# Spreading scores through DRAM, row sums by a column of ones, and a re-laid instruction order in a four-layer graph network

## The chip, the cores and the metric

The kernel runs on one core of one Trainium2 chip. The metric is device time in microseconds (us), from the start of the program to its end. A core has engines that each run their own queue of instructions in order and meet through semaphores: TensorE (PE, matrix products into PSUM; PEld are its weight loads), VectorE (DVE), ScalarE (ACT), GpSimd (POOL) and SyncE (SP, which here issues every DMA).

## The reference, cut to what matters

There are 128 graphs of 64 nodes with 512 features, all in float32. Four layers follow each other; each normalizes x, applies a ReLU, runs a graph layer on the result h, and adds it to x.

```python
h = relu(layernorm(x));  x = x + hypergraph_conv_twice(h, adj)          # layer 0, W1 512->1024, W2 1024->512
h = relu(layernorm(x))                                                   # layer 1
s = (h @ w) @ a
A = s[..., :, None] + s[..., None, :]
A = tanh(A / 8) * 8;  A = where(A >= 0, A, 0.1 * A);  A = exp(A) * adj
A = A / A.sum(-1, keepdims=True) * adj.sum(-1, keepdims=True)
x = x + A @ h @ w
h = relu(layernorm(x))                                                   # layer 2
weight = adj * exp((h @ Wq.T + bq) @ (h @ Wk.T + bk).T)
x = x + weight / weight.sum(2, keepdims=True) @ (h @ Wv.T + bv)
h = relu(layernorm(x))                                                   # layer 3
e = leaky_relu(sj[:, None, :] + si[:, :, None] + ab, 0.2)                # sj, si: h times two vectors
t = normalize_rows(adj * exp(e))
x = x + relu(sum over k of (t^k h) @ Wk[k] + bk[k])                      # k = 0, 1, 2
```

## The kernel before

**Tiles and groups.** Two graphs of 64 nodes fill the 128 partitions, and four such tiles (T = 4) are one group; there are NG = 16 groups. Small matrices of a group (adjacency, attention weights) are held in packed form, 128 x 4 x 64, or spread into block-diagonal 128 x 128 tiles ("bd") that a product can use. Layers 0 and 1 run over all 16 groups first, x then goes to DRAM (tensors xm), and layers 2 and 3 run over the 16 groups with other weights in the same memory (wa_mem, wb_mem).

**The large products.** They use a seven-product scheme (functions `strassen` and `seven`, products at L570 and L779): DVE combines operands (L562), PE forms seven products, ACT and DVE collect them in tiles U (L538, L540, L542), and a function of the layer evicts each result (for instance `scaled`, L588 and L590, for z in layer 0). Layers 0, 2 and 3 also transpose activations by an ACT copy into 16-bit planes, a DMA transpose (L519), and an ACT copy back (L520).

**Normalization.** `pre_ln` takes statistics on DVE (L489 to L491), a power on POOL (L492), one more small DVE operation (L499) and an ACT instruction (L500) that makes h. In layers 1 and 3 the four tiles h of a group are made once, multiplied with a vector for the scores (function `dot`, L358), and held until the softmax is done, when they are used again.

**Scores.** `bcast_sum` needs, for every pair of nodes of a graph, a row value plus a column value. It multiplies the column of values with an identity (dg, L605), lets PE sum over partitions with a block matrix of ones (ones_bd, L607), and adds the column to the result (L612). Layer 1 then forms the transposed attention matrix, and gets its row sums and those of the adjacency by two more products with ones_bd (L719), a reciprocal over 256 values per partition (L722) and a multiplication (L723), before it fills the block-diagonal tile PT (L725). Layer 2 gets its row sums by four one-column products (`col_sums`, L628), takes the reciprocal (L831), multiplies PT with the 512-wide value tile (L834), and scales and adds into x (L835). Layer 3 fills a transition tile tr (L858), transposes it (L863), squares it (L869), applies both powers to h (L883) and multiplies with three stacked weights.

**What sets the order.** Nothing is in program order. Every operation is entered in a graph (class `Graph`) with an engine, an estimated cost, its buffers and a due time (`prio`, advanced by `step`). `run` is a list scheduler: it goes through estimated time, starts on each engine what can start first, and among several the one with the lowest due time. It also picks the buffer slots. The instructions are then emitted in the order found, so each engine's queue is fixed when the kernel is built. The parameters are a stretch factor for each layer, a period for each loop, and a lead for the loads:

```python
STRETCH, PERIOD1, PERIOD2, LEAD = (1.65, 1.86, 2.69, 2.67), 80.0, 75.8, 1.5
```

The setup of layers 2 and 3 (Wq times Wk, L453 and L458; score vectors, L358 and L437) is entered with group 2 of the first loop. The estimate of a DMA is its size at 190 KB per us of queue time, and 2.0 us of latency.

Of the kernel before, what the change touches and what calls it, by code (L numbers as in the profile page):

```python
# [14 lines left out]
P = 128  # L15
C = 64
# [23 lines left out]
class Graph:  # L40
# [6 lines left out]
    def __init__(self):  # L47
        self.ops = []
        self.last_write, self.reads = {}, {}
        self.prio = 0.0  # L50

    def op(self, eng, cost, fn, r=(), w=()):
        o = Op()
        o.eng, o.cost, o.fn, o.prio = eng, cost, fn, self.prio
# [27 lines left out]
    def run(self, slots, after):  # L82
# [22 lines left out]
        while left:  # L105
# [42 lines left out]
            for q in o.succ:  # L148
                q.npre -= 1
                q.ready = max(q.ready, end if q.eng != o.eng else t + o.cost)  # L150
                if not q.npre:
                    open_[q.eng].append(q)
# [9 lines left out]
def tile_adj_preln_d4(  # L162
# [19 lines left out]
        "bd": ([P, T, P], 4), "dg": ([P, T, C], 1), "ee": ([P, T, C], 2),  # L182
        "st": ([P, 2, 6], 6), "mv": ([P, 2], 10), "ve": ([P, 1], 10), "rs": ([P, 1], 10), "nm": ([P, 1], 10),
        "col": ([P, T], 24), "ss": ([P, T, 2], 2),
# [6 lines left out]
        ([("s2", [P, 3, 4, P], 1), ("s1", [P, 3, 2, P], 2)], [("vu", [P, 2, D], 2), ("tt", [P, T, 2, P], 1)]),  # L191
# [57 lines left out]
    def c_v(n, from_psum=False):  # L249
        return n / 960 + 0.155  # L250
# [13 lines left out]
    def dma(kb, fn, r, w):  # L264
        return G.op("SP", kb / 190.0, fn, r, w)
# [4 lines left out]

    ident = const.tile([P, P], F32, name="ident")
    make_identity(nc, ident)
    ident2 = const.tile([P, C], F32, name="ident2")
    nc.vector.tensor_add(ident2, ident[:, :C], ident[:, C:])
    ones = const.tile([P, P], F32, name="ones")
    nc.vector.memset(ones, 1.0)
    ones_bd = const.tile([P, P], F32, name="ones_bd")
    nc.vector.memset(ones_bd, 0.0)
    for s in HALVES:
        nc.vector.memset(ones_bd[s, s], 1.0)  # L280
# [34 lines left out]
    xt, adjs, xmid = {}, {}, {}  # L315

    def load_group(g, src):
        b = Buf("adj")
        dma(256, lambda: nc.sync.dma_start(b.t, adj[g]), [], [b])
        adjs[g] = b  # L320
        for t in range(T):
            xx = Buf("x")
            at, key = src(g, t)
            dma(256, lambda xx=xx, at=at: nc.sync.dma_start(xx.t, at), key, [xx])
            xt[g, t] = xx
# [7 lines left out]

    G.prio = -1000.0
    load_group(0, x_in)
    load_w("w1", w1_sb, W1T)
    b1_b = [load_row(b1[i * D:(i + 1) * D]) for i in range(2)]
    gb2 = const.tile([P, KH, 2], F32, name="gb2")
    dma(8, lambda: nc.sync.dma_start(gb2[:, :, 0], gamma), [], ["gb2g"])
    dma(8, lambda: nc.sync.dma_start(gb2[:, :, 1], beta), [], ["gb2b"])  # L340
    load_w("w2", w2_sb, W2T)
    b2_b = load_row(b2)
    G.prio = 10.0
    load_w("w", w_sb, w)
    bq_c = load_cols("bq_c", bq, KD)
# [15 lines left out]
    def combine(name, w_, x_, kc, n, eng):  # L361
# [8 lines left out]
        G.op(eng, cost, lambda: sub(x_[:, 1], blk(1, 1), blk(0, 1)), [*low, *high], [(name, "x1")])  # L370
        G.op(eng, cost, lambda: sub(blk(0, 1), blk(0, 1), blk(0, 0)), [*low, (name, "x1")], [T1])
# [36 lines left out]
    def setup_l0():  # L408
# [6 lines left out]
        dve(0.2, lambda: nc.vector.tensor_scalar(gsc[:, :, 0], gb2[:, :, 0], 1.0 / DH, None, op0=ALU.mult), ["gb2g"], ["gsc0"])  # L415
        dve(0.2, lambda: nc.vector.tensor_copy(gsc[:, :, 1], gb2[:, :, 1]), ["gb2b"], ["gsc1"])
# [10 lines left out]
        for c in range(KH):  # L427
            dve(0.75, lambda c=c: nc.vector.scalar_tensor_tensor(
                w2_sb[:, c, :], w2_sb[:, c, :], gb2[:, c, 0:1], pm.t, op0=ALU.mult, op1=ALU.subtract),
                [pm, "gb2g"], [("w2", c // 2)])  # L430
# [9 lines left out]
    def setup_l1():  # L440
        wa, a_b = Buf("col"), temp(a.partition_broadcast(P))
        for c in range(KD):
            dot(lambda c=c: w_sb[:, c, :], lambda: a_b.t, lambda c=c: wa.t[:, c:c + 1], [("w", c // 2), a_b], [(wa, c)])
        spread(lambda: wa.t, lambda: wa_b.t, [(wa, c) for c in range(KD)], wa_b)

    def setup_l2():
# [3 lines left out]
        for o in range(KD):  # L450
            q_, k_ = temp(Wq[o * P:(o + 1) * P, :]), temp(Wk[o * P:(o + 1) * P, :])
# [8 lines left out]
            pe(c_mm(1, KD), mg, [k_, "bq_c"], [pg])  # L460
        for c in range(KD):
# [5 lines left out]
    def setup_l3():  # L467
        kk = Buf("mv")
        bv_t = temp(bv3.partition_broadcast(P))
        ab_t = load_tmp("rs", 1, lambda t: t, ab.partition_broadcast(P))  # L470
        for s in range(2):
            av, cc = temp(aw[s * D:(s + 1) * D].partition_broadcast(P)), Buf("col")
            dot(lambda: bv_t.t, lambda av=av: av.t, lambda s=s: kk.t[:, s:s + 1], [bv_t, av], [(kk, s)])
            for c in range(KD):
                wv = temp(Wv3[c * P:(c + 1) * P, :])
                dot(lambda wv=wv: wv.t, lambda av=av: av.t, lambda c=c, cc=cc: cc.t[:, c:c + 1], [wv, av], [(cc, c)])
            spread(lambda cc=cc: cc.t, lambda s=s: c3_b[:, s, :], [(cc, c) for c in range(KD)], ("c3", s))
# [7 lines left out]
    def norm_stats(src, k, r):  # L485
# [6 lines left out]
        pool(0.57, lambda: nc.gpsimd.tensor_tensor(rs.t, ve.t, mhalf, ALU.pow), [ve], [rs])  # L492
        return mv, rs

    def pre_ln(g, t):

        xx, nm, h = xt[g, t], Buf("nm"), Buf("h")
        mv, rs = norm_stats(lambda i: xx.t, 1, [xx])
        dve(0.16, lambda: nc.vector.scalar_tensor_tensor(nm.t, mv.t[:, 0:1], -1.0, rs.t, op0=ALU.mult, op1=ALU.mult), [mv, rs], [nm])  # L499
# [14 lines left out]
    def transposed(src, ksrc, planes, back, kback, dst, kdst):  # L514
# [4 lines left out]
        dma(200, lambda: nc.sync.dma_start_transpose(u16(back()).rearrange("p (b r) -> p b r", r=P), u16(planes.t)), [planes], kback)  # L519
# [64 lines left out]
    def scaled(dst, wdst, scale, ks, add, ka, p, u, v, n):  # L584

        if u is not None:
            (U, i), j, add0 = u, v[1], add
            dve(c_v(n), lambda: nc.vector.scalar_tensor_tensor(U.t[:, j], U.t[:, i], scale(), add0(), op0=ALU.mult, op1=ALU.add), [u, *ks, *ka], [v])  # L588
# [12 lines left out]

    def bcast_sum(col, row, r, extra=None):

        dg, p, z = Buf("dg"), Buf("ps"), Buf("ee")
        dve(0.42, lambda: nc.vector.tensor_mul(dg.t, ident2[:, None, :].to_broadcast([P, T, C]),  # L605
                                               row()[:, :, None].to_broadcast([P, T, C])), r, [dg])
        pe(c_mm(256, 1), lambda: nc.tensor.matmul(p.t[:, :T * C], ones_bd, dg.t.rearrange("p t c -> p (t c)"), start=True, stop=True), [dg], [p])  # L607
        if extra is not None:
# [3 lines left out]
        dve(0.42, lambda: nc.vector.tensor_add(z.t, p.t[:, :T * C].rearrange("p (t c) -> p t c", t=T),  # L612
                                               col()[:, :, None].to_broadcast([P, T, C])), [p, *r], [z])
# [8 lines left out]
    def col_sums(bd, r):  # L622

        p = Buf("ps")

        def mm():
            for t in range(T):
                nc.tensor.matmul(p.t[:, t:t + 1], bd.t[:, t, :], ones[:, 0:1], start=True, stop=True)  # L628
        pe(c_mm(1, T), mm, r, [p])
        return p  # L630


    def layer0(g):
        ad = adjs[g]
        AT = lambda: ad.t[:, 1]

        HT, mB, be, rb, pm, M = Buf("bd"), Buf("mB"), Buf("col"), Buf("col"), Buf("ps"), Buf("bd")
        for s in HALVES:
            dve(0.5, lambda s=s: nc.vector.tensor_scalar(HT.t[s, :, s], AT()[s], 0.0, None, op0=ALU.not_equal), [ad], [(HT, s.start)])
        dve(0.42, lambda: nc.vector.tensor_scalar(mB.t[:, :, :C], AT(), 0.0, None, op0=ALU.not_equal), [ad], [mB])  # L640
# [4 lines left out]
        dve(0.16, lambda: nc.vector.tensor_copy(mB.t[:, :, C:], AT()[:, :, 0:1]), [ad], [mB])  # L645
# [15 lines left out]
        for t0 in (0, 2):  # L661
            mh, zs, ys, rTs = [], [], [], []
            for t in (t0, t0 + 1):
                xx = xt[g, t]
                h = pre_ln(g, t)
                pool(1.3, lambda xx=xx, h=h: nc.gpsimd.tensor_add(xx.t, xx.t, h.t), [h, xx], [xx])  # L666
# [351 lines left out]
```

## Time and profile before

| | |
|---|---|
| time, median of 3 | 2472.81 us (2470.64 to 2474.09) |
| span of the profiled execution | 2471.6 us |
| mean granted TensorE clock | 0.992 |
| DMA moved | 163.39 MB, mean 66 GB/s |
| h made in all four layers (L500) | 256 instructions, 208.0 us busy on ACT |
| powers on POOL (L492) | 320 instructions, 202.2 us busy |

A group of instructions in the profile is a line of the kernel, an engine, an operation, what it writes and reads, its shape and count; then its busy time, the mean time of one, and after a second bar the idle time of the engine just before it, with what ended the idle time. A float32 matmul appears as two instructions. Matmuls overlap in the pipe, so the mean time of one is longer than what it adds to the span.

### The profile page before, as it was taken

How to read it: one execution, taken by the hardware profiler on the slowest of the kernel's cores; microseconds unless marked ns; L12 is line 12 of the kernel's file. 1: busy time of each engine (PE TensorE's matmuls, PEld its weight loads, DVE VectorE, ACT ScalarE, POOL GpSimd, SP SyncE). 2: the span in 40 equal slices, each digit the busy share in tenths (PEclk: the TensorE clock that was granted, in tenths of full speed). 3: DMA queues.
4: the chain of work that ended last, by engine and by line, in shares of the span. 5: the costliest groups of instructions: out<-in, count | busy, mean ns of one | idle time of the engine just before them, and what ended most of it. 6: DMA issues, size and time to landing. Idle time of an engine off the chain costs nothing.

```text
span 2471.6 us, 32994 instructions
## 1 busy us (share of the span) xinstructions
PE 2416.3 (98%) x12058; PEld 1878.4 (76%) x12058; DVE 1808.8 (73%) x4128; ACT 1176.1 (48%) x1626; POOL 723.9 (29%) x842
## 2 busy tenths in 40 slices
PE   8999999999999999999989999999999999999998
PEld 4566767776677776677777888888888888888886
DVE  8678888888888888888875566665566665566663
ACT  4355554655554555454633445343445343445321
POOL 3223344333444333444221212221212221212220
PEclk9989999999999999999999999999999999999998
DMA  5242222222222222222431233212223222222211
GB/s 187 68 103 52 60 59 66 73 56 49 63 64 61 73 56 52 60 69 56 120 111 46 58 69 69 69 43 61 55 69 73 61 48 60 56 69 67 58 22 34
DMA packets 323698, 163.39 MB, mean 66 GB/s; under 512 B 278096, under 2 KB 278096, under 8 KB 323536
## 3 DMA queue, kind: packets, MB, share of 16 engines
q1 hardware_dynamic: 323536, 161.28, 26.3%
q8 instruction: 95, 1.56, 0.3%
q14 instruction: 67, 0.55, 0.1%
HBM read 59.52 MB, written 34.60 MB: 38 GB/s over the span
## 4 chain that ended last, share of the span: by engine, by line
PE 86%; DVE 9%; ACT 2%; DMA 1%; issue 1%; POOL 0%; DVEq 0%; ACTq 0%; POOLq 0%
PE ps L570 56%; PE ps L779 15%; PE ps L509 3%; PE ps L883 2%; PE ps L834 2%; PE ps L697 2%; DVE s_s_vu_tt L562 2%; PE ps L804 2%; DVE rT_a L562 1%; DVE u L588 1%; PE ps L607 1%; DVE ee L722 1%; PE ps L869 1%; DVE z_hT L590 1%; ACT rT_a L520 1%
## 5 line engine op out<-in xcount | busy, mean ns | idle before, releaser
L570 PE MATMUL ps<-wb_mem,rT_a 128*128 128x256 f32 x2056 | 480.7, 382 | 8.1 <-ACT rT_a L520 4.5
L492 POOL TENSOR_TENSOR rs<-ve,mhalf 128x1 f32<-128x1 f32 x320 | 202.2, 634 | 919.9 <-DVE ve L491 841.3
L570 PEld LDWEIGHTS ps<-wb_mem,rT_a 128*128 128x128 f32 x2056 | 389.5, 191 | 80.6 <-issue 13.8
L500 ACT ACTIVATE h<-x,nm,rs 128x512 f32<-128x512 f32 x256 | 208.0, 815 | 319.0 <-DVE nm L499 309.0
L570 PE MATMUL ps<-wb_mem,s_s_vu_tt 128*128 128x256 f32 x1152 | 274.3, 381 | 1.2 <-DVE x L737 0.9
L570 PE MATMUL ps<-wb_mem,tmp_mB_s 128*128 128x256 f32 x1152 | 263.1, 380 | 0.0
L570 PEld LDWEIGHTS ps<-wb_mem,s_s_vu_tt 128*128 128x128 f32 x1152 | 219.0, 191 | 48.3 <-issue 14.4
L570 PE MATMUL ps<-wb_mem,mT_a 128*128 128x256 f32 x1016 | 246.8, 382 | 5.7 <-DVE y_qT L600 5.0
L570 PE MATMUL ps<-wa_mem,mT_a 128*128 128x512 f32 x512 | 244.5, 602 | 2.8 <-ACT mT_a L511 1.5
L570 PEld LDWEIGHTS ps<-wb_mem,tmp_mB_s 128*128 128x128 f32 x1152 | 217.8, 190 | 37.0 <-issue 7.2
L570 PEld LDWEIGHTS ps<-wb_mem,mT_a 128*128 128x128 f32 x1016 | 188.7, 190 | 48.5 <-DVE y_qT L600 13.2
L538 ACT COPY u<-ps 128x256 f32<-128x256 f32 (+1 forms) x160 | 73.1, 457 | 277.7 <-PE ps L570 227.1
L570 PE MATMUL ps<-wa_mem,s_s_vu_tt 128*128 128x512 f32 x384 | 181.0, 595 | 1.5 <-DVE z_hT L590 1.0
L489 DVE BATCH_NORM_STATS2 st<-x 128x6 f32<-128x512 f32 x256 | 175.1, 684 | 3.6 <-DMA x<-xm 3.0
L570 PEld LDWEIGHTS ps<-wa_mem,mT_a 128*128 128x128 f32 x512 | 94.7, 192 | 95.5 <-issue 85.6
L896 POOL TENSOR_TENSOR u<-u,bk_b 128x256 f32<-128x256 f32 x96 | 79.1, 823 | 300.9 <-DVE u L542 177.8
L540 DVE TENSOR_TENSOR u<-ps,u 128x256 f32<-128x256 f32 (+1 forms) x160 | 84.5, 528 | 104.4 <-PE ps L570 44.3
L520 ACT COPY rT_a<-z_hT 128x1024 uint16<-128x1024 uint16 x128 | 145.9, 1160 | 15.5 <-DMA z_hT<-tmp_mB_s 15.4
L509 PEld LDWEIGHTS ps<-bd,h 128*128 128x128 f32 x1024 | 129.5, 195 | 24.1 <-issue 10.8
L518 ACT COPY o<-h 128x1024 uint16<-128x1024 uint16 x128 | 133.3, 1041 | 22.9 <-DVE o L358 21.3
L677 ACT ACTIVATE z_hT<-z_hT 128x512 f32<-128x512 f32 x128 | 80.5, 630 | 127.5 <-DVE z_hT L590 124.0
L666 POOL TENSOR_TENSOR x<-x,h 128x512 f32<-128x512 f32 x64 | 91.1, 1423 | 169.2 <-ACT h L500 168.9
(181 smaller groups left out, 4242.6 us busy)
## 6 DMA issues: line engine op xcount, KB each, us to landing
x<-in_x_dram SPq DMA_DIRECT2D x64, 256.0 KB, 2.7
xm<-x SPq DMA_DIRECT2D x64, 256.0 KB, 2.0
x<-xm SPq DMA_DIRECT2D x64, 256.0 KB, 2.8
out_dram<-x SPq DMA_DIRECT2D x64, 256.0 KB, 2.0
adj<-in_adj_dram SPq DMA_DIRECT2D x32, 256.0 KB, 2.9
wb_mem<-in_Wk_dram SPq DMA_DIRECT2D x6, 512.0 KB, 6.6
wa_mem<-in_W1T_dram SPq DMA_DIRECT2D x2, 1024.0 KB, 8.5
wb_mem<-in_W2T_dram SPq DMA_DIRECT2D x4, 512.0 KB, 6.2
```

The lines of the kernel that those rows point to most:

```text
L489: dve(0.69, lambda i=i: nc.vector.bn_stats(st.t[:, i, :], src(i)), [r[i]], [(st, i)])
L492: pool(0.57, lambda: nc.gpsimd.tensor_tensor(rs.t, ve.t, mhalf, ALU.pow), [ve], [rs])
L500: act(0.82, lambda: nc.scalar.activation(h.t, xx.t, AF.Relu, bias=nm.t, scale=rs.t), [xx, nm, rs], [h])
L509: nc.tensor.matmul(quad(p)[:, c, :], h.t[:, c * P:(c + 1) * P], rhs(), start=True, stop=True)
L518: act(1.05, lambda: nc.scalar.copy(u16(planes.t).rearrange("p (q c) -> p q c", q=2), u16(src()).rearrange("p (c q) -> p q c", q=2)), ksrc, ...
L520: act(1.16, lambda: nc.scalar.copy(u16(dst()).rearrange("p c (k q) -> p c k q", q=2), u16(back()).rearrange("p (q c r) -> p c r q", q=2, c ...
L540: dve(c_v(n), lambda: nc.vector.tensor_add(at(1)(), p2.t[:, :n], at(0)()), [p2, (U, 0)], [(U, 1)])
L570: nc.tensor.matmul(p.t[:, :n], lhs()[:, c, :], rhs(c), start=first and c == 0, stop=c == kc - 1, skip_group_check=True)
L666: pool(1.3, lambda xx=xx, h=h: nc.gpsimd.tensor_add(xx.t, xx.t, h.t), [h, xx], [xx])
L677: act(0.63, lambda: nc.scalar.activation(z.t[:, cols], z.t[:, cols], AF.Relu), [(z, j)], [(z, j)])
L779: nc.tensor.matmul(pair(p.t)[:, o, :], a, b, start=first and o == 0 and c == 0, stop=c == 1, skip_group_check=True)
L896: pool(0.75, lambda: nc.gpsimd.tensor_add(U.t[:, iv], U.t[:, u[1]], add()), [u, ka], [v])
```

## The change

It has four parts.

1. **Scores through DRAM.** A function `across` writes a packed column of values (128 x 4) to a small DRAM tensor and reads it back so that each partition holds the values of all 64 nodes of its graph (tile rw). `bcast_sum` adds to that directly, and layer 1 gets the row factor of its attention matrix in the same way, after forming the sums on DVE in the packed, untransposed form. The products with ones_bd are no longer needed.
2. **Sums by a column of ones.** The value tile of layer 2 gets a 513th column of ones in its middle, so that the product with PT carries the row sum with it. The product is split into two halves, with an own PSUM tile each.
3. **h twice.** In layers 1 and 3 the statistics are kept and h is made once for the scores and again for the products, so that no h tile is held across the softmax.
4. **The order.** Costs are closer to measured ones (issue time and landing of DMAs apart, a DMA's successor on the same queue waits for the landing), each part of a layer gets its own offset on the due time (`part`, table AT), and the setup of layers 2 and 3 is entered at the beginning. Gamma and beta are stored so that they load in contiguous pieces.

```diff
-                q.ready = max(q.ready, end if q.eng != o.eng else t + o.cost)
+                q.ready = max(q.ready, t + o.cost if q.eng == o.eng != "SP" else end)
...
-    def dma(kb, fn, r, w):
-        return G.op("SP", kb / 190.0, fn, r, w)
+    def dma(kb, fn, r, w, issue=0.34):
+        return G.op("SP", max(kb / 380.0, issue), fn, r, w)
...
+    def part(name):
+        G.shift = AT[name]
...
-    gb2 = const.tile([P, KH, 2], F32, name="gb2")
+    gb2 = const.tile([P, 2, KH], F32, name="gb2")
...
+    def across(col, r):
+        b = Buf("rw")
+        d = dram.tile([P, T], F32, name=f"row{len(rows)}")
+        key = ("row", len(rows))
+        rows.append(d)
+        dma(4, lambda: nc.sync.dma_start(d, col()), r, [key])
+
+        def back():
+            for s in HALVES:
+                nc.sync.dma_start(b.t[s].rearrange("p c t -> p (c t)"), d[s].rearrange("c t -> (c t)").partition_broadcast(C))
+        dma(128, back, [key], [b], 1.2)
+        return b
...
     def bcast_sum(col, row, r, extra=None):
-        dve(0.42, lambda: nc.vector.tensor_mul(dg.t, ident2[:, None, :].to_broadcast([P, T, C]),
-                                               row()[:, :, None].to_broadcast([P, T, C])), r, [dg])
-        pe(c_mm(256, 1), lambda: nc.tensor.matmul(p.t[:, :T * C], ones_bd, dg.t.rearrange("p t c -> p (t c)"), start=True, stop=True), [dg], [p])
+        b, z = across(row, r), Buf("ee")
...
+        dve(0.61, lambda: nc.vector.tensor_add(z.t, by_node(b), col()[:, :, None].to_broadcast([P, T, C])), [b, *r], [z])
...
     def layer1(g):
+        stats = [pre_stats(g, t) for t in range(T)]
         for t in range(T):
-            h = pre_ln(g, t)
+            h = pre_ln(g, t, stats[t])
...
-                nc.tensor.matmul(pd.t[:, i * T * C:(i + 1) * T * C], ones_bd, m().rearrange("p t c -> p (t c)"), start=True, stop=True)
-        dve(2.0, lambda: nc.vector.reciprocal(rn.t, half(0)), [pd], [rn])
-        dve(0.42, lambda: nc.vector.tensor_mul(rn.t, rn.t, half(1)), [pd, rn], [rn])
+        dve(0.42, lambda: nc.vector.tensor_reduce(num.t, ad.t[:, 0], AX.X, ALU.add), [ad], [num])
+        dve(0.42, lambda: nc.vector.tensor_mul(zz.t, z.t, ad.t[:, 0]), [z, ad], [zz])
+        dve(0.42, lambda: nc.vector.tensor_reduce(den.t, zz.t, AX.X, ALU.add), [zz], [den])
+        dve(0.16, lambda: nc.vector.reciprocal(den.t, den.t), [den], [den])
+        dve(0.16, lambda: nc.vector.tensor_mul(den.t, den.t, num.t), [den, num], [den])
+        rn = across(lambda: den.t, [den])
...
-            ph = [left_mul_T(hs[t], lambda t=t: PT.t[:, t, :], PTk, "mT") for t in (t0, t0 + 1)]
+            ph = [left_mul_T(pre_ln(g, t, stats[t]), lambda t=t: PT.t[:, t, :], PTk, "mT") for t in (t0, t0 + 1)]
...
     def layer2(g):
-        pd, rd = col_sums(PT, PTk), Buf("col")
-        dve(0.18, lambda: nc.vector.reciprocal(rd.t, pd.t[:, :T]), [pd], [rd])
...
+            for j, (c0, c1) in enumerate(((0, D // 2 + 1), (D // 2 + 1, D + 1))):
+                pe(c_mm(256, 1), lambda p=ps[j], t=t, v_=v_, c0=c0, c1=c1: nc.tensor.matmul(
+                    p.t[:, :c1 - c0], PT.t[:, t, :], v_.t[:, t % 2, c0:c1], start=True, stop=True),
+                   [*PTk, (v_, j)] + ([(v_, 2)] if j == 0 else []), [ps[j]])
+            dve(0.16, lambda p=ps[0], rd=rd: nc.vector.reciprocal(rd.t, p.t[:, D // 2:D // 2 + 1]), [ps[0]], [rd])
...
-    STRETCH, PERIOD1, PERIOD2, LEAD = (1.65, 1.86, 2.69, 2.67), 80.0, 75.8, 1.5
+    STRETCH, PERIOD1, PERIOD2 = (1.62, 0.5, 2.98, 1.93), 88.03, 82.78
+    setup_l2()
...
-        if g == 2:
-            G.prio = g * PERIOD1
-            setup_l2()
-            setup_l3()
```

## The prediction

> **What bounds the kernel now.** I read the busy shares first, then the same shares by stretch, then the groups of matmuls, and last the order of time where TensorE (PE) stands still.
>
> ```profile
> PE 2416.3 (98%) x12058; PEld 1878.4 (76%) x12058; DVE 1808.8 (73%) x4128; ACT 1176.1 (48%) x1626; POOL 723.9 (29%) x842
> ```
>
> PE is busy for 2416.3 of 2471.6 us, so it stands still for 55.3 us in all. The stretches show where (length, then PE, PEld, DVE, ACT, POOL busy, clock, DMA share):
>
> ```profile
> 0.00:150.00 150.00, 128.73 (x423) 74.75 (x424) 113.31 (x253) 63.26 (x89) 44.31 (x53) 0.97 0.42 125
> 150.00:1230.00 1080.00, 1069.88 (x4521) 775.56 (x4521) 911.97 (x2105) 598.55 (x844) 403.69 (x463) 1.00 0.27 65
> 1230.00:1304.00 74.00, 63.20 (x349) 51.71 (x349) 56.64 (x135) 35.03 (x48) 18.66 (x25) 0.95 0.37 105
> 1304.00:2410.00 1106.00, 1104.72 (x6513) 933.73 (x6513) 704.61 (x1591) 469.39 (x630) 252.91 (x295) 1.00 0.25 58
> 2410.00:2472.00 62.00, 49.75 (x257) 42.66 (x255) 22.30 (x48) 9.89 (x16) 4.35 (x6) 0.88 0.11 34
> ```
>
> Idle PE, by subtraction: 21.3 us at the start, 10.1 us in the loop of layers 0 and 1, 10.8 us at the switch to layers 2 and 3, 1.3 us in the second loop, 12.2 us at the end. Inside the loops PE is the bound almost without a gap, so only less PE work makes them shorter. The three ends are bound by latency, and there an order can win. VectorE (DVE) is at 84% in the first loop (911.97 of 1080), so it is the engine that can become the next bound there.
>
> The matmuls that the change takes away, and the ones it splits:
>
> ```profile
> L834 PE MATMUL ps<-s_s_vu_tt,bd 128*128 128x512 f32 x128 | 61.2, 602 | 0.0
> L607 PE MATMUL ps<-dg,ones_bd 128*128 128x256 f32 x64 | 21.0, 411 | 2.8 <-DVE dg L605 2.8
> L628 PE MATMUL ps<-ones,bd 128*128 128x1 f32 x128 | 15.2, 240 | 0.0
> L719 PE MATMUL ps<-adj,ones_bd 128*128 128x256 f32 x32 | 9.5, 379 | 0.0
> L719 PE MATMUL ps<-ee,ones_bd 128*128 128x256 f32 x32 | 9.5, 379 | 0.0
> ```
>
> Every f32 matmul is two instructions, and the mean (602, 411, 379 ns) includes the pipe, so the price is the distance between starts:
>
> ```profile
> 732.07 0.59 PE L607 MATMUL ps<-dg,ones_bd 128*128 128x256 f32 x2
> 732.50 1.00 PE L650 MATMUL ps<-tmp_mB_s,bd 128*128 128x65 f32 x8
> ...
> 736.87 0.59 PE L719 MATMUL ps<-ee,ones_bd 128*128 128x256 f32 x2
> 737.30 0.59 PE L719 MATMUL ps<-adj,ones_bd 128*128 128x256 f32 x2
> ```
>
> A 256-wide pair takes 0.43 us (732.07 to 732.50). The end shows the latency chain of the last group, with nothing else left to run (idle before in brackets):
>
> ```profile
> 2415.00 0.70 PE L607 MATMUL ps<-dg,ones_bd 128*128 128x256 f32 x2 [2.76 <-DVE dg L605]
> 2419.34 1.11 PE L863 MATMUL ps<-ident,bd 128*128 128x128 f32 x4 [3.64 <-DVE bd L858]
> 2421.13 2.08 PE L869 MATMUL ps<-s_s_vu_tt,bd 128*128 128x128 f32 x8 [0.68 <-ACT s_s_vu_tt L865]
> 2423.88 5.50 PE L883 MATMUL ps<-s_s_vu_tt,h 64*128 64x128 f32 x48 [0.68 <-ACT s_s_vu_tt L871]
> ```
>
> **What the Trainium skill says.** "TensorE: Matmul & The Clock Gate", Part 1: after about 3.4 us of idleness the array runs at half clock until it has been busy for about as long. The trace agrees: L869 takes 2.08 us here after the gap, while 128 instructions are busy for 18.0 us in all, or 1.1 us per eight. A gap therefore costs more than its length. The same page (section on the array's architecture) calls DVE and ACT strict FIFO: a DVE instruction waiting for a DMA holds everything behind it. "DMA: Bandwidth & Descriptors", Anatomy of one DMA: a fixed cost of about 2.0 us, mostly the receipt. The trace agrees: xm<-x lands after a median 2.0 us, x<-xm after 2.8.
>
> **The change, part by part.**
>
> *PE work.* L607 goes: 32 pairs at 0.43 = 13.8 us. Both sums at L719 go: 32 pairs at 0.43 = 13.9 us. The four one-column products at L628 go: they start at 2392.21 and the next group at 2393.02, so 0.81 us by 16 groups = 13.0 us. L834 becomes two halves, of 257 and 256 columns. Eight 512-wide instructions run 3.44 us (3.60 busy less the 0.16 overlap seen at every group's end); sixteen 256-wide ones at 0.215 take 3.44 us, and the extra column under 1 ns each. So 0. Sum **-40.7 us**, all on the bounding engine.
>
> *The replacement.* `across` writes the packed scores to DRAM and reads them back to all partitions, twice per group in layer 1, once in layer 3. That is 48 round trips of one write and two reads, on the SP queue. No row shows a hop, so I bound it. Low: write 2.0, issue of the second read 0.4, read 2.8, semaphores 0.1 = 5.3 us. High: the small loads bq_c (6.1 us) and ab (5.7) behind full queues plus 0.4 = 12.2 us. I take 5.5: DMA share in the loops is 0.25, and bq_c stood in the crowded start. In the built order of the changed kernel, DVE has 8 instructions between the last dot product and the first user of the first hop: two U scalings and three z evictions at 0.75 us, three statistics at 0.69, 5.8 us together. For the second hop it has 5.4 us (a 0.42 multiply, two 0.42 combinations, two sums into U at 0.69, three scalings at 0.75, small ones 0.5). So a 5.5 us hop is just covered, a 12.2 us one is late by 6.4 and 6.8. Behind the waiting DVE instruction stand z evictions and Strassen sums for which PE waits. In layer 3 about 5 us are covered and DVE is at 64%, so I put nothing there. On SP one transpose may stand behind a write; ACT feeds it well ahead, so nothing.
>
> *DVE.* Layer 1 loses the 1.76 us reciprocal, a 0.42 multiply and the 0.42 spread, gains two reductions and a multiply at 0.42 and small ones of 0.33, and three operations read the transposed row: 0.42 to 0.84 each (0.84 is the slow form of L813); I take 0.6. Net -0.5 us per group. Layer 2: four evictions at 0.75 plus 0.18 become 4 x (0.18 + 2 x 0.48) = 4.6, +1.4 us, hidden at 64%.
>
> *ACT.* h twice in layers 1 and 3: 128 more at 0.81 = 104 us, so 1176 to 1280 us of 2472. Hidden: 52% busy. It frees h slots that were held across the softmax. POOL gets 32 one-column memsets, hidden.
>
> *Order at the end.* The built order puts L863, L869 and the last L883 between blocks of layer 3's Strassen products, 12 instructions or 2.6 us each. The gaps shown are 7.8 us, and half clock stretches the four groups and the first product by about 4. Of 12 I count **-10**.
>
> *Order at the switch.* The gaps are 6.5, 3.0, 1.1 and 0.2 us, plus about 4 of half clock. In the new order layer 1's last products are mixed into the first layer-2 group, and 3.4 us of PE work lie between the last reader of the first hT and the next group's first product, which needs two 1.16 us ACT copies. I count **-9** of 15.
>
> *Order at the start.* Wq and Wk now come first and their 18.8 us of products replace the piece that left gaps of 8.9 us between 100 and 150. But W1's 2 MB and adj queue behind them: at about 400 GB/s, which the busiest 2 us stretches of the start show, adj lands near 14 us instead of 3, and DVE combines W1 before the mask. PE then has early gaps of about 14 us instead of 9.7. Gamma and beta, whose 4-byte pieces held the queue 4.5 us, get cheap. Net **-4**, uncertain by 12.
>
> *In the loops* I add **+6** for hops that come late now and then. 2472.8 - 40.7 - 10 - 9 - 4 + 6 = **2415**.
>
> **The rivals.** (1) As above: 2415, chance 0.50. (2) Less work, but the boundaries stay: start +8, switch -3: 2472.8 - 40.7 - 10 - 3 + 8 + 6 = 2433, 0.17. For it: the first 20 us are DMA-bound (84% share). (3) Hops of about 8 us: late by 5 us per layer-1 group on DVE, half reaching PE: 16 x 2.5 = 40 instead of 6, so 2449, 0.15. For it: DVE at 84%; against: DMA share 0.25. (4) All gaps close, -12 end, -13 switch, -15 start, 0 in the loops: 2392, 0.12. (5) Hops at 12.2 us: 13.2 us late per group, more than DVE's 16% slack of some 12 us; half reaches PE, 16 x 6.6 = 106: 2472.8 - 40.7 - 23 + 106 = 2515, slower than before, 0.06. Against it: nothing but the crowded start shows such landings.
>
> **How the numbers follow.** The likeliest is (1). Range 2396 to 2447: it leaves out (5), about half of (3) and half of (4), about 0.2. Faster than by 0.2%: all but (5) = 0.93, with 0.01 for a mixture at no change.
>
> **What would show it.** PE busy near 2375 us with 128 fewer instructions; PE idle in 150 to 1230 still near 10 to 16 us; no gap above 1 us before the final transposes; landings of the row write and read near 2 and 2.5 us; ACT near 1280. It would be wrong if DVE waits for rw by several us per group, if W1 products start far later than the 17.7 us of now, or if transposes queue behind row reads.

## The result, and the profile after

The changed kernel takes 2440.73 us (median of 4 runs, 2438.0 to 2443.39) beside 2472.39 us of the kernel before (4 runs, 2470.64 to 2474.09). The ratio is **0.9872, 95% interval 0.9855 to 0.9889**: 1.3% faster. The forecast was 2415. That lies inside the forecast range of 2396 to 2447, and 26 us above its sum. TensorE lost the work that was forecast, but the two loops gave back more than the ends won. The first line of the page:

```profile
PE 2381.8 (98%) x11930; PEld 1851.8 (76%) x11930; DVE 1836.4 (75%) x4252; ACT 1265.6 (52%) x1754; POOL 723.3 (30%) x874
```

There are 128 fewer matmul instructions, and PE is busy 34.5 us less. The same by stretch (length, then PE, PEld, DVE, ACT, POOL busy, clock, DMA share, GB/s):

```profile
0.00:150.00 150.00, 130.10 (x441) 75.95 (x442) 118.52 (x263) 70.82 (x101) 43.73 (x54) 0.95 0.42 126
150.00:1230.00 1080.00, 1061.21 (x4428) 755.52 (x4427) 915.07 (x2135) 639.15 (x899) 396.85 (x464) 1.00 0.28 68
1230.00:1304.00 74.00, 70.55 (x405) 59.60 (x405) 56.13 (x138) 37.87 (x51) 24.66 (x31) 0.98 0.42 108
1304.00:2380.00 1076.00, 1065.13 (x6362) 913.68 (x6360) 722.53 (x1672) 505.24 (x686) 251.42 (x317) 1.00 0.27 61
2380.00:2440.00 60.00, 54.76 (x301) 47.08 (x299) 24.14 (x48) 12.49 (x19) 6.62 (x9) 1.00 0.15 42
```

By subtraction PE now stands still for 19.9, 18.8, 3.5, 10.9 and 5.2 us. Before it was 21.3, 10.1, 10.8, 1.3 and 12.2. (The fourth stretch was 30 us longer before.) So the gaps at the switch and the end closed for the most part, and the loops, which had few, opened. The end, in order of time (start, duration, idle before in brackets):

```profile
2387.55 0.66 PE L914 MATMUL ps<-ident,bd 128*128 128x128 f32 x4 [0.48 <-DVE bd L907]
2388.04 2.82 PE L594 MATMUL ps<-wb_mem,mT_a 128*128 128x256 f32 x12
2390.70 1.05 PE L920 MATMUL ps<-s_s_vu_tt,bd 128*128 128x128 f32 x8
...
2394.27 2.95 PE L935 MATMUL ps<-s_s_vu_tt,h 64*128 64x128 f32 x48
```

L914, L920 and L935 are the old L863, L869 and L883. Twelve instructions of Strassen products now stand between them, and of the gaps of 3.64, 0.68 and 0.68 us one of 0.48 is left. L920 takes 1.05 us instead of 2.08.

Busy PE is not PE at its peak, so I made a **ledger**. For every kind of matmul I took the median distance from its start to the next start, and multiplied it by the count; every pass between the products that use half of the array (L804 and L883, now L843 and L935) and the others adds 0.1 us, since the first start after a pass comes 0.09 to 0.14 us late in both kernels. That is the work. The rest of a stage's length is loss, visible gap or not. The stages are cut at products, so that they hold the same groups in both kernels: loop 1 from the last L697/L730 of the second group to that of the fifteenth (13 groups), loop 2 likewise between the last P V products.

| stage | before: length, work, loss | after: length, work, loss | change of loss |
|---|---|---|---|
| start, groups 1 and 2 | 204.5, 168.2, 36.3 | 192.2, 160.8, 31.4 | -4.9 |
| loop 1, 13 groups | 960.9, 947.7, 13.2 | 964.3, 933.5, 30.8 | **+17.6** |
| switch | 193.7, 173.6, 20.1 | 180.8, 165.0, 15.7 | -4.4 |
| loop 2, 13 groups | 965.5, 952.0, 13.5 | 961.6, 937.9, 23.7 | **+10.2** |
| end | 147.0, 128.3, 18.6 | 140.9, 131.1, 9.8 | -8.8 |

The work falls by 41.5 us (2369.8 to 2328.3), and the losses rise by 9.7. Loop 1 has 14 us less work and is 3.4 us longer. That is the question for the experiments.

Where loop 1 loses is seen in any of its groups. First SP's DMA queue, then one line each of PE, ACT and DVE from the same 10 us:

```profile
431.35 0.33 SPq L632 DMA_DIRECT2D row<-col  x1
431.72 1.14 SPq L329 DMA_DIRECT2D adj<-in_adj_dram  x1
432.91 1.27 SPq L543 DMA_TRANSPOSE z_hT<-tmp_mB_s  x1
434.29 1.15 SPq L636 DMA_DIRECT2D rw<-row  x2
```

```profile
438.33 1.99 PE L594 MATMUL ps<-wb_mem,rT_a 128*128 128x256 f32 x8 [0.36 <-ACT rT_a L544]
```

```profile
437.12 1.16 ACT L544 COPY rT_a<-z_hT 128x1024 uint16<-128x1024 uint16 x1 [0.86 <-DMA z_hT<-tmp_mB_s]
```

```profile
437.85 1.27 DVE L759 TENSOR_TENSOR bd<-ee,rw 64x256 f32<-64x256 f32 x2 [1.13 <-DMA rw<-row]
```

Two things are late. The write of the row is issued at 431.35, and DVE can use the row at 437.85: a hop of 6.5 us, of which the work in between covers 5.4, and DVE stands for 1.13. And the transpose issued at 432.91 lands only at 437.1, so that W2's first product waits for its copy rT. Both fell in the time of one load of adj and two row reads. Over all 48 hops the time from the write's issue to the landing of the second read has a median of 5.3 us; the second hop of layer 1, shown here, has 6.8 in the first loop.

### The profile page after: what moved, and what is told of

The parts are those of the page before. It is cut to its first block, busy times and chain, and to the rows that moved or that the text cites. A ratio compares the mean times of both kernels' runs of the same rounds, so it can differ in the third digit from the quotient of the medians.

```text
span 2439.8 us, 33261 instructions
## 1 busy us (share of the span) xinstructions
PE 2381.8 (98%) x11930; PEld 1851.8 (76%) x11930; DVE 1836.4 (75%) x4252; ACT 1265.6 (52%) x1754; POOL 723.3 (30%) x874
## 4 chain that ended last, share of the span: by engine, by line
PE 71%; DVE 14%; DMA 7%; ACT 5%; issue 3%; SPq 0%; POOL 0%; DVEq 0%; ACTq 0%
PE ps L594 48%; PE ps L817 12%; PE ps L533 3%; DMA z_hT<-tmp_mB_s 3%; PE ps L935 2%; DVE s_s_vu_tt L586 2%; DVE st L507 2%; PE ps L878 2%; DMA rw<-row 1%; PE ps L730 1%; DVE nm L517 1%; ACT h L524 1%; ACT rT_a L544 1%; DVE s_s_vu_tt L868 1%; DVE x L731 1%
## 5 line engine op out<-in xcount | busy, mean ns | idle before, releaser
L524 ACT ACTIVATE h<-x,nm,rs 128x512 f32<-128x512 f32 x384 | 303.1, 811 | 541.3 <-DVE nm L517 490.2
L510 POOL TENSOR_TENSOR rs<-ve,mhalf 128x1 f32<-128x1 f32 x320 | 199.2, 624 | 692.6 <-DVE ve L509 605.6
L594 PEld LDWEIGHTS ps<-wb_mem,tmp_mB_s 128*128 128x128 f32 x1152 | 217.5, 190 | 30.8 <-DVE tmp_mB_s L586 1.8
L562 ACT COPY u<-ps 128x256 f32<-128x256 f32 (+1 forms) x160 | 73.0, 456 | 200.0 <-PE ps L594 153.6
L533 PEld LDWEIGHTS ps<-bd,h 128*128 128x128 f32 x1024 | 129.0, 193 | 33.6 <-issue 13.6
L695 POOL TENSOR_TENSOR x<-x,h 128x512 f32<-128x512 f32 x64 | 86.2, 1346 | 194.0 <-ACT h L524 194.0
L952 DVE TENSOR_TENSOR u<-ps,u 128x256 f32<-128x256 f32 x96 | 40.6, 423 | 136.3 <-PE ps L594 121.6
L533 PE MATMUL ps<-bd,h 128*128 128x128 f32 x1024 | 132.2, 278 | 3.6 <-DVE bd L759 1.5
```

Source lines behind the costliest of these rows:

```text
L510: pool(0.65, lambda: nc.gpsimd.tensor_tensor(rs.t, ve.t, mhalf, ALU.pow), [ve], [rs])
L524: act(0.82, lambda: nc.scalar.activation(h.t, xx.t, AF.Relu, bias=nm.t, scale=rs.t), [xx, nm, rs], [h])
L533: nc.tensor.matmul(quad(p)[:, c, :], h.t[:, c * P:(c + 1) * P], rhs(), start=True, stop=True)
L562: act(n / 1200 + 0.17, lambda: nc.scalar.copy(at(0)(), p1.t[:, :n]), [p1], [(U, 0)])
L594: nc.tensor.matmul(p.t[:, :n], lhs()[:, c, :], rhs(c), start=first and c == 0, stop=c == kc - 1, skip_group_check=True)
L695: pool(1.43, lambda xx=xx, h=h: nc.gpsimd.tensor_add(xx.t, xx.t, h.t), [h, xx], [xx])
```

## The experiments

All ran against the kernel before; the ratio is to it. The five lengths are the ledger's stages, from each profile. The start varies by some 4 us between profiles of the same order (6 with e7), and 192.2 of the changed kernel is its longest value, so read the loops. Loop 1 is 964.3 us again in e4 and e8, whose edits lie in the other loop: its length repeats well.

| kernel | median us | ratio, 95% interval | start | loop 1 | switch | loop 2 | end |
|---|---|---|---|---|---|---|---|
| before | 2472.4 | | 204.5 | 960.9 | 193.7 | 965.5 | 147.0 |
| changed | 2440.7 | 0.9872 (0.9855-0.9889) | 192.2 | 964.3 | 180.8 | 961.6 | 140.9 |
| e1 order only | 2512.7 | 1.0169 (1.0155-1.0183) | 194.9 | 986.0 | 193.8 | 981.6 | 153.4 |
| e2 parts only | 2674.3 | 1.0827 (1.0808-1.0847) | 205.0 | 1065.7 | 205.8 | 1039.2 | 158.8 |
| e3 no hop | 2427.4 | 0.9822 (0.9808-0.9835) | 188.8 | 953.0 | 178.8 | 963.2 | 141.7 |
| e4 ones once | 2437.2 | 0.9862 (0.9848-0.9875) | 190.1 | 964.3 | 179.9 | 959.8 | 140.9 |
| e5 hop unused | 2434.7 | 0.9856 (0.9842-0.9869) | 189.6 | 960.4 | 178.6 | 962.4 | 141.3 |
| e6 h thrice | 2462.5 | 0.9966 (0.9955-0.9978) | 191.6 | 971.5 | 183.2 | 972.4 | 144.4 |
| e7 GpSimd narrow | 2412.8 | 0.9766 (0.9752-0.9779) | 185.8 | 947.6 | 178.5 | 958.9 | 140.6 |
| e8 P V narrow | 2440.6 | 0.9884 (0.9869-0.9899) | 188.4 | 964.3 | 180.3 | 962.6 | 140.9 |
| e9 before, GpSimd narrow | 2457.1 | 0.9942 (0.9928-0.9956) | 199.1 | 949.6 | 194.0 | 965.8 | 147.3 |
| e10 second h narrow | 2433.6 | 0.9847 (0.9833-0.9860) | 188.8 | 965.1 | 179.4 | 959.8 | 140.1 |
| e11 reads on ACT's queue | 2445.9 | 0.9900 (0.9887-0.9914) | 189.6 | 967.5 | 182.0 | 962.6 | 140.9 |
| e12 adj later | 2439.3 | 0.9873 (0.9856-0.9889) | 189.4 | 967.6 | 179.8 | 960.3 | 140.9 |

### e1 and e2: the order alone, and the parts alone

e1 takes the changed kernel and puts the old computation back into it:

```diff
-        b, z = across(row, r), Buf("ee")
...
+        pe(c_mm(256, 1), lambda: nc.tensor.matmul(p.t[:, :T * C], ones_bd, ...), [dg], [p])
...
-            h = pre_ln(g, t, stats[t])          # the second one, layers 1 and 3
+            h = hs[t]
...
-            for j, (c0, c1) in enumerate(((0, D // 2 + 1), (D // 2 + 1, D + 1))):
...
+        pd, rd = col_sums(PT, PTk), Buf("col")
```

> The order, costs and due times of the changed kernel with the computation of the kernel before (scores spread by TensorE products with ones_bd, sums by four one-column products, h made once and held). Ledger of the traces before and after: TensorE work -41.5 us, start -5, switch -4, end -9, first loop +17.6, second loop +10.2. Theory P (the loops lose time because of the new parts: DRAM hops, h twice, halves of P V): the loops stay as before and the order alone gives 2472 - 5 - 4 - 9 = about 2454, between 2450 and 2460. Theory O (the loops lose time because of the new order, whichever way scores are spread): 2472 - 18 + 28 = about 2482, at least 2472, so not faster than the kernel before.

e2 takes the kernel before and puts the three parts into it; AT, the new costs and the new rule for what is ready stay out.

> The three parts of the change (hops, ones column, h twice) in the order parameters, costs and due times of the kernel before. Theory P: TensorE work -41 us, loops +28 or more because the old costs know nothing of a hop: 2472 - 41 + 28 = about 2459 or later. Theory O: -41 and nothing lost in the loops, start, switch and end as before: about 2432. A value near 2445 would say that both carry part of it.

Neither theory holds in both runs: P fails in e1, and O, which holds there (at least 2472), fails in e2 by 240 us. The order alone is 1.7% slower than the kernel before, the parts alone 8.3% slower, and together they are 1.3% faster. So the gain of the order does not come without the parts that it was laid for: in e1 the end is 6.4 us longer than before and the switch as long as before, though the changed kernel won 6 and 13 us there. In e2 VectorE waits for rows (us in total, times, longest; L626 and L728 are the changed kernel's L650 and L759):

```profile
DVE ee L626 <- DMA rw<-row: 78.8, 32, 6.2
...
DVE bd L728 <- DMA rw<-row: 64.0, 19, 5.0
```

That is 142.8 us of waiting for rows, against 27.3 us in the changed kernel (19.2 in L759 and 8.1 in L650). The hops themselves are no longer: a median of 5.3 us from the write's issue to the second landing, as in the changed kernel. A hop that the order does not cover is dear: loop 1 of e2 is 101 us longer than the changed kernel's, 7.8 us per group, though not all of that need be the rows. The old planner lets a read follow its write at once on SP and books a hop at 0.02 + 0.67 + 2.0 = 2.7 us; that this is why the order of e2 is so bad is read from the code, and was not tried by itself.

The other runs therefore keep the changed kernel's order and alter one thing in its place.

### e3 and e5: what the hops cost, and how

```diff
-        dma(4, lambda: nc.sync.dma_start(d, col()), r, [key])
+        dma(4, lambda: None, r, [key])
...
-                nc.sync.dma_start(b.t[s].rearrange("p c t -> p (c t)"), d[s]...)
+                pass
...
-        return b.t[s].rearrange("p c t -> p t c")
+        return slots["rw"][0][s].rearrange("p c t -> p t c")
```

> The changed kernel with every instruction in its place but all 48 DRAM hops left out: the row is never written or read back, and the sums and PT read one constant tile instead (other values, same shapes). If the hops cause what the first loop lost (VectorE waiting for the row, transposes held behind the row reads on the SP queue): 17 us there and a part of the 10 in the second loop come back, 2440 - 20 = about 2420 or less. If the loops lose by the order of VectorE and ScalarE work or by the shared port of VectorE and GpSimd: 2436 to 2440.

e5 leaves the DMAs and changes only the last line, to a constant tile.

> The changed kernel with all 48 hops still written and read back on the SP queue in their places, but the sums and PT read one constant tile, so that no VectorE instruction waits for a row. Leaving the hops out altogether gave 2427.4 us, 13 less than the changed kernel. Theory V (the 13 us are VectorE waiting for the row, 27 us in the trace, with evictions behind it that TensorE needs): again about 2427. Theory Q (they are the SP queue: the row read waits for the row write to land and holds the transposes behind it, so that rT and the second layer's first product come late): about 2440, as with hops.

Without hops loop 1 falls by 11.3 us (964.3 to 953.0), loop 2 does not fall, and the whole is 13 us shorter. With hops that nobody waits for it falls by 3.9. So in loop 1 VectorE's waiting is worth 3.9 us, and the other 7.4 come from what the DMAs do to something else. PE's wait for rT (us in total, times, longest) shows what, in the changed kernel, in e5 and in e3:

```profile
PE ps L594 <- ACT rT_a L544: 8.4, 14, 1.9
```

```profile
PE ps L594 <- ACT rT_a L544: 8.5, 13, 1.8
```

```profile
PE ps L594 <- ACT rT_a L544: 2.2, 2, 1.2
```

Neither theory was right alone.

### e11: is it the queue?

```diff
-                nc.sync.dma_start(b.t[s].rearrange("p c t -> p (c t)"), d[s]...)
+                nc.scalar.dma_start(b.t[s].rearrange("p c t -> p (c t)"), d[s]...)
```

> The changed kernel with the row reads of the hops issued from ScalarE's DMA queue instead of SP's, at the same place in the planned order; the result is the same. Theory Q (about half of the 13 us of the hops is SP waiting for the row write to land, with transposes behind it; the run with unread hops kept 7 of them): SP is never held, TensorE's wait of 8 us for rT (L544) goes, 2431 to 2435. Rival: ScalarE reaches the read before the row has landed and is held itself, with h, rT and u copies behind it, at 0.2 us or more of the time for each us: 2440 to 2450.

It takes 2445.9 us, not less (the intervals of e11 and of the changed kernel just touch): with the reads away from SP, PE's wait for rT grows to 13.6 us. Part of this is the rival of the expectation: ScalarE is held 1.1 us by the issue of two reads, and in 5 of the waits, 4.4 us, its copy comes late behind its own other work. But the waits in which the copy itself stood for a transpose to land did not shrink either, 8.0 us after 7.2 in the changed kernel. So the read that holds the SP queue is not the cause. The landings of the 104 transposes of loop 1 say more. After more than 4.5 us land: before 2, changed 15, e3 3, e5 14, e11 24. In the changed kernel 19 take over 4 us: 16 of them have the adj load and row reads beside them, the other three only transposes. A transpose usually lands after 2.8 us, and adj after 2.8 without hops and 4.3 with them. So they seem to hinder each other below the queues, in the DMA engines; e12 tests that.

### e12: taking the transfers apart

The changed kernel with the one change of e4 below (the column of ones written once), and each adj load of loop 1 after the row read:

```diff
-        dma(256, lambda: nc.sync.dma_start(b.t, adj[g]), [], [b])
+        dma(256, lambda: nc.sync.dma_start(b.t, adj[g]), [("read", 2 * min(g - 3 + NG * (src is x_mid), NG - 1) + 1)], [b])
...
-        dma(128, back, [key], [b], 1.2)
+        dma(128, back, [key], [b, ("read", len(rows) - 1)], 1.2)
```

> The changed kernel with the column of ones written once (that alone gave 2437.2 us) and with each adj load of the first loop, which stands between a row write and its read on the SP queue, moved two transposes behind the read; the planner then moves the mask operations that use it (L667 to L673) some evictions later on VectorE, TensorE's order is the same. The result is the same. Theory D (what the hops cost beside VectorE's wait is a collision in the DMA engines: in the traces with hops 14 to 24 of 104 transposes of the first loop land after more than 4.5 us, each beside a row read and an adj load, without hops 3, whichever queue issues the reads): the late transposes fall to a few, TensorE's wait of 8 us for rT goes, about 2430. Rival: adj now comes too late for the masks, which are needed at once, and what is won at rT is lost at M (L678) and behind VectorE's wait: 2437 to 2445.

The mechanism holds, and the gain is gone all the same. Transposes over 4.5 us fall from 15 to 2, adj lands after 3.2 us instead of 4.3, and rT is hardly waited for any more (the first two lines are the waits of PE, the last of DVE, all of e12):

```profile
PE ps L594 <- DVE z_hT L614: 9.7, 8, 1.8
...
PE ps L594 <- ACT rT_a L544: 2.4, 2, 1.2
```

```profile
DVE bd L667 <- DMA adj<-in_adj_dram: 23.9, 13, 3.8
```

But the masks need adj at once. VectorE now stands at L667, the z evictions (L614) wait behind it in its queue, and PE waits for those. Loop 1 is 967.6 us, 3.3 longer than in e4. The rival of its expectation came true.

### e7 and e9: VectorE beside GpSimd

```diff
-                nc.gpsimd.tensor_add(xx.t, xx.t, h.t)          # and x + b2, and the U sums of V, L866
+                nc.gpsimd.tensor_add(xx.t[:, :8], xx.t[:, :8], h.t[:, :8])
```

> The changed kernel with three GpSimd additions cut to 8 columns, in their places: x + h and x + b2 of layer 0 (L695, L696) and the U sums of V in layer 2 (L866); the rest of those sums is left out. Theory S (VectorE's combinations L586 and the multiply L853 take up to three times their time while GpSimd works on them, and so VectorE's results come late): L586 128x256 falls from 0.64 to about 0.43 us in the first loop, L853 from 1.12 to about 0.6, and the time falls by 6 us in the first loop and up to 6 in the second: 2428 to 2434. If VectorE's slack hides this: 2438 to 2441.

> The kernel before with the same three GpSimd additions cut to 8 columns as in the changed kernel's run that gained 28 us (17 of them in the first loop); the rest of those sums is left out. Theory S' (the new order laid GpSimd's additions beside VectorE's combinations more than the old one, so that the loss in the first loop is new contention for the shared port): here the same cut gains little, at most some 12 us in all and 5 in the first loop, about 2460 to 2467. Theory S'' (the contention was there before as well and cost the same): it gains about as much here, 2443 to 2450, and the loss of the first loop lies elsewhere.

In the changed kernel this takes 28 us away, more than theory S had, and in the kernel before 15, between the two theories of e9. Loop 1 falls by 16.7 and by 11.3 us, so **5.4 us** of loop 1's loss are contention that the new order added, and the larger part was there before. VectorE is busy 1836.4 us in the changed kernel and 1745.9 in e7, 1808.8 before and 1748.8 in e9. Its groups show where, first of the kernel before, then of the changed kernel, then of e7 (busy us, mean ns, idle before):

```profile
L562 DVE TENSOR_TENSOR s_s_vu_tt<-mT_a 128x256 f32<-128x256 f32 x64 | 30.8, 481 | 4.6 <-ACT mT_a L511 4.0
...
L813 DVE TENSOR_TENSOR bd<-ee,adj 64x256 f32<-64x256 f32 x32 | 26.6, 830 | 3.8 <-ACT ee L812 2.4
```

```profile
L586 DVE TENSOR_TENSOR s_s_vu_tt<-mT_a 128x256 f32<-128x256 f32 x64 | 40.9, 638 | 7.2 <-ACT mT_a L535 6.9
...
L853 DVE TENSOR_TENSOR bd<-ee,adj 64x256 f32<-64x256 f32 x32 | 35.9, 1123 | 8.4 <-ACT ee L852 7.9
```

```profile
L586 DVE TENSOR_TENSOR s_s_vu_tt<-mT_a 128x256 f32<-128x256 f32 x64 | 28.2, 441 | 7.5 <-ACT mT_a L535 6.4
...
L853 DVE TENSOR_TENSOR bd<-ee,adj 64x256 f32<-64x256 f32 x32 | 13.4, 420 | 8.3 <-ACT ee L852 7.8
```

One pair of instructions in the changed kernel, GpSimd's and VectorE's:

```profile
556.83 1.27 POOL L695 TENSOR_TENSOR x<-x,h 128x512 f32<-128x512 f32 x1
```

```profile
557.07 1.31 DVE L586 TENSOR_TENSOR s_s_vu_tt<-mT_a 128x256 f32<-128x256 f32 x1
```

An instruction of 0.42 us takes 1.31, about as long as the addition beside it. The Trainium skill, "SBUF — State Buffer", section "SBUF: two separate sides", says why: VectorE with two SBUF inputs and GpSimd share a port pair, which the first one holds for its whole instruction. The trace agrees: of the 64 instructions of this group in the changed kernel the 13 that run beside L695 and L696 take 1.31 us each, and the 35 with no addition beside them 0.42. L853 takes 1.22 us in the 28 that run beside L866 and 0.41 in the other 4. L813 before, whose 0.83 us the prediction called a slow form, is the same case: 29 of its 32 run beside another GpSimd addition (L896), which e9 left whole. A rival would be that shorter additions only bring their own sums earlier; but what waits for GpSimd hardly moves, the longest, VectorE's wait for rs (L510), from 22.3 to 22.2 us.

### e6 and e10: h made twice

```diff
-        act(0.82, lambda: nc.scalar.activation(h.t, xx.t, AF.Relu, bias=nm.t, scale=rs.t), ...)
+        act(0.82, lambda: [nc.scalar.activation(h.t, xx.t, AF.Relu, ...) for _ in range(n)], ...)   # n = 2 for the second h
```

> The changed kernel with every second h of layers 1 and 3 written twice over in a row, with the same values: ScalarE gets 128 more activations of 0.81 us, 104 us in all, just what the change had added; nothing else moves. Theory A (h made twice delays the ScalarE copies that TensorE waits for, rT at L544 and u at L562, and this makes up the rest of the loops' loss, some 6 us in the first loop and 10 in the second): a third copy costs as much again or more, 2455 us or later. If the second h is hidden as predicted: 2439 to 2444.

e10 writes `h.t[:, :8]` in the second h instead, and its readers take constant tiles.

> The changed kernel with the second h of layers 1 and 3 cut to 8 columns, everything in its place; TensorE and the transposes take constant tiles instead (other values). ScalarE gets rid of some 128 x 0.6 = 77 us. A third copy cost 22 us, or 0.22 us for each us put on ScalarE. Theory A (the loops pay for the second copy at the same rate): 77 x 0.22 = 17 us less, about 2424. If only further load hurts and the second copy itself fits into slack: 2436 to 2441.

A third copy puts 97 us on ScalarE (1265.6 to 1362.7) and costs 21.7, as theory A had it: +7.2 in loop 1, +10.8 in loop 2. Taking most of the second away (ScalarE 1265.6 to 1209.7 us busy, 56 less instead of the 77 that I had reckoned) gives 7.1 us in all, at the edge of what the intervals tell apart and between the two forecasts: +0.8 in loop 1, -1.8 in loop 2, and the rest mostly in the start, where profiles differ by as much. So the second copy fits into ScalarE's slack in loop 1, as predicted, and a further one would not. I should not have carried the price of more load over to less.

### e4 and e8: the rest of loop 2

> The changed kernel with the column of ones written for the first group of layer 2 alone (the two buffers keep it, since the evictions of V write only the other columns): 30 of the 32 small GpSimd memsets go, and with them 63 us in which GpSimd stood waiting for the P V products of the group before. If that wait, with the rs and U sums queued behind it, is what costs the second loop its 10 us: about 2432. If the memset is hidden: 2438 to 2441.

> The changed kernel with the second of the two evictions of each P V (L884) cut to 8 columns: 64 x 0.3 = some 20 us less on VectorE in the second loop; half of layer 2's result is not added to x. Theory E (the split evictions, 4.6 instead of 3.2 us per group, make VectorE late in the second loop): the loop wins most of its 10 us, about 2431. If they are hidden as predicted: 2438 to 2441.

```diff
-            pool(0.2, lambda v_=v_: nc.gpsimd.memset(v_.t[:, :, D // 2:D // 2 + 1], 1.0), [], [(v_, 2)])
+            pool(0.2, lambda v_=v_: nc.gpsimd.memset(...) if g == 0 else None, [], [(v_, 2)])
```

e4 shortens loop 2 by 1.8 us. Its interval overlaps with the changed kernel's, so that it is better is likely but not shown. e8 changes nothing: the split evictions of P V are hidden, as predicted.

Where loop 2 loses can be read from the distances between PE's starts, as in the ledger. The wait before the second half of P V is new (one group, first PE, then VectorE):

```profile
1481.15 1.97 PE L878 MATMUL ps<-s_s_vu_tt,bd 128*128 128x256 f32 x8 [0.30 <-DVE ve L881]
```

```profile
1477.02 2.46 DVE L853 TENSOR_TENSOR bd<-ee,adj 64x256 f32<-64x256 f32 x2 [0.58 <-ACT ee L852]
1479.51 1.49 DVE L868 TENSOR_TENSOR s_s_vu_tt<-ps,u 128x512 f32<-128x512 f32 x2
```

The value tile (L868) comes late behind the slowed multiply L853, and PE loses 6.0 us here in 13 groups; 2.2 are left in e7, 4.8 in e4. In 12 groups layer 2's products wait for the copy u (L562), 4.9 us with the pass that falls there, about 3.4 without it; e4 leaves 4.0 of the 4.9 and e10 3.6. Layer 2's products among themselves (L817) lose 6.4 us instead of 3.2, in every run that keeps this order but e6, where it is 7.5; why is open.

## Why the prediction was right in its range, and which term failed

Its sum was 2472.8 - 40.7 - 10 - 9 - 4 + 6 = 2415. The ledger gives 2472.8 - 41.5 - 8.8 - 4.4 - 4.9 + 27.8 = 2441.0, and 2440.7 was measured. The direction and the range held, but the gain is 32 us instead of 58. That the range held is in part luck: its upper half was left for boundaries that stay or for hops of 8 us, and neither came. Term by term:

- **PE work, -40.7: right.** It measured -41.5. A pair at 0.43 us was the right price, and the 257-wide halves cost nothing more than the whole.
- **Order at the end, -10: right.** It measured -8.8, and the gaps closed as the built order showed. But it is not the order's alone: with the old parts (e1) the end got longer.
- **Order at the start, -4: right**, -4.9, and up to 4 us more in other profiles of the same order.
- **Order at the switch, -9: half of it.** It measured -4.4. The gaps that the prediction named closed (10.8 to 3.5 us in that stretch). But over the ledger's longer stage the visible gaps fall only from 12.7 to 8.9 us: outside that stretch they grow from 1.9 to 5.4.
- **The loops, +6: the step that failed.** They lost 27.8 us, 17.6 and 10.2, and this is 22 of the 26 us of error. The hop was close: a median of 5.3 us, 6.5 in the group shown, where 5.5 was taken, and the 5.4 us of VectorE work that I counted as cover are the 5.4 us that the trace shows. What failed is that I asked only who waits for the row. e3 prices the hops at 11.3 us in loop 1; only 3.9 of them are VectorE's wait (e5), and 7.4 come from the transfers, transposes that land late beside row reads and adj (e11, e12). For these I had written "so nothing", with the queue alone in mind. The new order adds 5.4 us of contention between VectorE and GpSimd (e7 against e9), which I had not looked for, though VectorE's 84% stood in the prediction. Together 16.7 of 17.6. The two were not taken away together, but they act for the most part on different waits. By the distances between starts PE loses 9.3 us before products that wait for rT in loop 1, 1.1 in e3 and 8.5 in e7; and 6.9 us before those that wait for VectorE's y_qT and u (L624, L566), 7.7 in e3 and nothing in e7. Only some 2.4 us before products that wait for ScalarE's u (L562) go in both, so that the sum may count these twice.
- **Loop 2, 10.2 us**, is placed by the trace: 6.0 before the second half of P V, 3.4 in waits for u, 3.2 within layer 2's products, less some 2.4 that other products won. The experiments give back 2.7 (e7, where the same cut gave nothing in the kernel before), 1.8 (e4) and 1.8 (e10) of it, some 6 us, with stages that differ by 1 us between like profiles; the hops and the evictions give nothing (e3, e8). The passes between half-array products and others are no cause: 154 before and 155 after. The rest stays open.

The signs that were named: PE is busy 2381.8 us (near 2375), ScalarE 1265.6 (near 1280), the write lands after 1.4 us and the read after 3.2 (2 and 2.5; the write is below the fixed cost of 2.0 that I had started from), no gap over 1 us stands before the last transposes, and PE's idle time from 150 to 1230 is 18.8 us where 10 to 16 was to show the loops right. VectorE rose by 27.6 us instead of some 14; the contention is the reason, L586 128x256 (up 26 us in all its four forms) and L853 (9.3 us more than L813 had). Of the signs of being wrong, one came: W1's first product starts at 37.1 us instead of 17.7, and the start is shorter all the same. VectorE waits for rw by 1.7 us per group, 27.3 in all, not by several.

The rivals nearest in time are those of 2433 (boundaries that stay) and 2449 (hops of 8 us), each 8 us off, and each for a reason that did not act.

## What to carry to other kernels

When the bounding engine gets less work, ask of every stage whether a second engine is near its limit, and what shares a port with it: with VectorE at 84%, waits for transfers and for GpSimd reached TensorE, and 14 us of saved matmuls left loop 1 no shorter. Price a new DMA three times: its own latency, who stands in the queue behind its user, and which transfers it slows in the DMA engines. A hand-fitted order and the work it was fitted to can't be booked apart: test each in the other's absence before crediting either.

## What the hardware showed that I had not expected

A DRAM hop of one 2 KB column is cheap for DMA, 1.4 us for the write and 3.2 us for each read to 64 partitions (medians), but it takes adj from 2.8 to 4.3 us and single transposes from 2.8 to over 4.5. Moving its reads to another queue made more of the transposes late (24 instead of 15), not fewer. And three GpSimd additions, whose sums no matmul waits for in the list of waits, cost the changed kernel 28 us by making VectorE's instructions beside them up to three times as long, more than twice what all hops cost (13 us).
